# The seam between two layers: the last block's normalization moves to ScalarE, its products are shared out, and the second layer's buffers and loads are untied from the first

## The chip, the cores and the metric

The program runs on one core of a Trainium2 chip. The metric is the time of one execution in microseconds of the device. Three runs of the kernel before took 5094.03, 5087.31 and 5103.36 us; the median is 5094.03 us. Besides, one execution was recorded by the hardware profiler. Times with two decimals in the text are us from the start of its span.

In the profile PE is TensorE, DVE is VectorE, ACT is ScalarE, POOL is GpSimd and SP is SyncE, which here only issues DMAs. All work is recorded through a helper, so nearly all instructions carry its line, L158, and are told apart by the tiles that they write and read.

## The reference

The input x is 4 images of 64 channels and 256 x 256 pixels, float32. Two layers are applied, each with a group normalization ahead of it (32 groups of two channels) and a residual around it:

```
x = x + L0(group_norm(x))
x = x + L1(group_norm(x))
```

L0 raises the channels from 64 to 384 (a 1x1 convolution), runs a 3x3 depthwise convolution, and splits the result into q, k and v of 128 channels. Patches of 8 x 8 pixels of q and k are convolved circularly, `out = irfft2(rfft2(q) * rfft2(k))`. For each pixel `out` is normalized over its 128 channels: `(out - mu) / sqrt(var + 1e-5) * ln_w + ln_b`. It is multiplied by v and brought back to 64 channels.

L1 walks over the 256 columns of the image. Column w is computed from column w - 1 by a GRU cell, whose input is the three neighbouring pixels of the column before and whose state is the own column. The columns depend on each other, one after the other. The group normalization ahead of L1 needs the mean and the variance of all of layer 0's output, so nothing of L1 can be normalized before the last pixel of layer 0 is there.

## The kernel before, in words

Layer 0 works through 32 blocks (`NBLK`), each of 32 rows of one image and 64 patches per half (`NJ`). A block takes these stages, and stages of neighbouring blocks are interleaved by hand: `gated`, `project`, `add_residual` and `leave` of block n - 1 stand among the stages of block n. The order on each engine is the program's order (class `InOrder`).

- `pointwise` and `transform`: matmuls for q and k; `products` and `inverse` give `z`, the circular convolution, 128 x 64 x 128.
- `values` (eight groups, k = 0 to 7): matmuls for v into PSUM, which `keep_values` copies into the tile `v` on ScalarE: groups 0-1, 2, 3-4, 5 and 6-7. `psum(4)` and `psum()` hand out PSUM banks in a ring of eight, `place`, so a group can start only when an earlier one's copy has emptied its banks.
- `layer_norm` is a generator; `go()` runs a step of it between other stages. It takes the statistics of z, makes `mean` and `rstd` for each pixel, then scales: for each quarter of z two passes of VectorE over 128x2048 (`scaled`: subtract the mean, multiply by rstd), eight in all, and then `turned`, four transposes of z and four of v, each 128x2048.
- `gated`: ScalarE applies ln_w and ln_b to a quarter of z, and GpSimd multiplies the quarter of v by it, 128x2048.
- `project`: 32 matmuls for half a block (u = 0 or 1), summing the four quarters in PSUM.
- `residual` loads the input into slots 6 and 2 of the tile `wk` on SP's queue; `add_residual` adds it to the projection on VectorE; `leave` takes its statistics (bn_stats) and stores it to the DRAM tensor `x1` on POOL's queue.

After the loop there is a round for the last block alone (`if last:`). There `norm` is run to its end, all four quarters are gated and multiplied, and only then come, for u = 0 and again for u = 1, load, projection, add, statistics and store.

Between the layers `norm_of_blocks` combines the 32 blocks' statistics: a small reduction, a matmul with a matrix that averages (`avg4`), small operations on VectorE, a second matmul, a square root on ScalarE, a reciprocal, and a series of copies that bring mean and rstd into the two layouts that even and odd columns use (`sc1`).

The GRU's buffers are allocated after layer 0's are given back, and take their place: `raws` (16 raw columns), `xns`, `xts`, `stcols`. Layer 0's pool `big` held h, z, v, wk and other tiles together, and a tile that takes the place of a pool waits for everything that used it. `load_column` reads x1 on SP's queue, 16 columns ahead; `normalize` scales a column on ScalarE; `column` has the matmuls and `state` the gates of a column.

Of the kernel before, what the change touches and what calls it, by code (L numbers as in the profile page):

```python
# [18 lines left out]
P = 128  # L19
# [9 lines left out]
NJ = 64  # L29
# [76 lines left out]
    yield  # L106


def norm_of_blocks(nc, tmp, pool, psum, mv, eps, avg4):


    n = NBLK // B
    mean = pool.tile([P, NPAIR], F32, tag="gn1_mean", name="gn1_mean")
    rstd = pool.tile([P, NPAIR], F32, tag="gn1_rstd", name="gn1_rstd")
    m_all = tmp.tile([P, NBLK], F32, tag="m_all", name="m_all")
    d = tmp.tile([P, NBLK], F32, tag="d_all", name="d_all")
    m4 = tmp.tile([P, B], F32, tag="m4", name="m4")
    nc.vector.tensor_copy(m_all, mv[:, :, 0])
    nc.vector.tensor_reduce(
        m4, m_all.rearrange("p (b n) -> p b n", n=n), mybir.AxisListType.X, ALU.add  # L120
    )
    pm = psum.tile([P, B], F32, tag="gn", name="gn1_pm")
    nc.tensor.matmul(pm, lhsT=avg4, rhs=m4, start=True, stop=True)
    nc.vector.tensor_copy(m4, pm)
    nc.vector.tensor_tensor(
        d.rearrange("p (b n) -> p b n", n=n),
        m_all.rearrange("p (b n) -> p b n", n=n),
        m4.rearrange("p (b x) -> p b x", x=1).to_broadcast([P, B, n]),
        ALU.subtract,
    )  # L130
    nc.vector.tensor_tensor(d, d, d, ALU.mult)
    nc.vector.tensor_tensor(d, d, mv[:, :, 1], ALU.add)
    v4 = tmp.tile([P, B], F32, tag="v4", name="v4")
    nc.vector.tensor_reduce(v4, d.rearrange("p (b n) -> p b n", n=n), mybir.AxisListType.X, ALU.add)
    pv = psum.tile([P, B], F32, tag="gn", name="gn1_pv")
    nc.tensor.matmul(pv, lhsT=avg4, rhs=v4, start=True, stop=True)
    nc.scalar.activation(v4, pv, AF.Sqrt, bias=eps, scale=1.0)
    nc.vector.reciprocal(v4, v4)
    for b in range(B):
        at = slice((b % 2) * C, (b % 2) * C + C)  # L140
        nc.vector.tensor_copy(mean[at, b // 2 : b // 2 + 1], m4[at, b : b + 1])
        nc.vector.tensor_copy(rstd[at, b // 2 : b // 2 + 1], v4[at, b : b + 1])
    return mean, rstd


class InOrder:
# [17 lines left out]
def tile_conv_then_gru(  # L164
# [17 lines left out]

    const = ctx.enter_context(tc.tile_pool(name="const", bufs=1))
    dram = ctx.enter_context(tc.tile_pool(name="dram", bufs=1, space=DRAM))
    x1 = dram.tile([B, C, W, H], F32, tag="x1", name="x1")


    t_all = dram.tile([3, ROWS, 8, 16 * NS], F32, tag="t_all", name="t_all")
# [22 lines left out]
    st1 = const.tile([P, NBLK, 2], F32, tag="st1", name="st1")  # L211
    st1 = const.tile([P, NBLK, 2], F32, tag="st1", name="st1")
    with layer0 as s:
        big = s.enter_context(tc.tile_pool(name="big", bufs=1))
        tp = s.enter_context(tc.tile_pool(name="tp", bufs=4))
        ps2 = s.enter_context(tc.tile_pool(name="ps2", bufs=1, space=PSUM))
# [6 lines left out]
            place[0] = (at + banks) % 8  # L223
            return ring[:, at % 8 : at % 8 + banks]

        hx = big.tile([P, P * NP], F32, tag="h", name="h")
        h = hx[0:HALO].rearrange("p (c n) -> p c n", n=NP)
        z = big.tile([P, NJ, E], F32, tag="z", name="z")
        v = big.tile([P, NJ, E], F32, tag="v", name="v")
# [237 lines left out]
        def keep_values(k, count, pv):  # L467
            nc.scalar.copy(
                v[:, :, 16 * k : 16 * (k + count)], pv.rearrange("p x (f n) -> p n (x f)", n=NJ)
            )  # L470

        def layer_norm(n):

            st = lnst[:, 0:384].rearrange("p (a i k) -> p a i k", a=2, k=6)
# [37 lines left out]
                    )  # L512
                    yield

            def turned(of, i):
                chunk = of[:, :, 32 * i : 32 * i + 32]
                nc.vector.transpose(chunk, chunk)

            for i in range(4):
                yield from scaled(i)  # L520
            for i in range(4):
                turned(z, i)
                yield
                turned(v, i)
                yield

        def gated(n, i):
            f = slice(32 * i, 32 * i + 32)
            nc.scalar.activation(
                z[:, :, f],  # L530
                z[:, :, f],
                AF.Identity,
                bias=ln_sb[:, 1, i : i + 1],
                scale=ln_sb[:, 0, i : i + 1],
            )
            nc.gpsimd.tensor_tensor(v[:, :, f], v[:, :, f], z[:, :, f], ALU.mult)

        bn = {}

        def residual(n, u):  # L540
            b, r0 = n // 8, (n % 8) * 32 + u * 8
            xr = [wk[:, i].rearrange("p (r c) -> p r c", c=P) for i in (6, 2)]
            for g in range(2):
                for s in range(2):
                    nc.sync.dma_start(
                        xr[g][s * C : (s + 1) * C],
                        x[b, :, r0 + 16 * g : r0 + 16 * g + 8, s * P : s * P + P],
                    )
            return xr
# [26 lines left out]
                        ALU.add,  # L576
                    )

        def leave(n, u, xr):

            b, r0 = n // 8, (n % 8) * 32 + u * 8
            if u == 0:
                bn[n] = big.tile([P, 8, 6], F32, tag="bn", name=f"bn_{n}")
            for g in range(2):
                flat = xr[g].rearrange("p r c -> p (r c)")
                for p in range(2):
                    nc.vector.bn_stats(bn[n][:, 4 * u + 2 * g + p, :], flat[:, p * 512 : (p + 1) * 512])
                for s in range(2):
                    nc.gpsimd.dma_start(
                        x1[b, :, r0 + 16 * g : r0 + 16 * g + 8, s * P : s * P + P],  # L590
                        xr[g][s * C : (s + 1) * C],
                    )
            if u == 1:
                nc.vector.bn_aggr(st1[:, n, :], bn.pop(n))
# [22 lines left out]
        for n in range(NBLK + 1):  # L617
            last = n == NBLK
            more = not last and n // 8 + 1 < B
            if last:  # L620
                for _ in norm:
                    pass
                for i in range(4):
                    gated(n - 1, i)
                for u in range(2):
                    xr = residual(n - 1, u)
                    add_residual(u, project(n - 1, u), xr)
                    leave(n - 1, u, xr)
                break
            if more:  # L630
                look(n, 0)
# [51 lines left out]
            for unit in range(16):  # L683
                pointwise(n, 2, unit, unit in (4, 6, 15))
                if more and unit == 2:
                    count(n, 12)
                    if n % 8 == 7:
                        t = wk[:, 3]
                        nc.gpsimd.dma_start(t[:, 0 : 2 * P].rearrange("p (a q) -> p a q", a=2), sums)
                        image = norm_of_pieces(nc, st0, t, lambda: psum()[:, :, 0], eps, sc0[:, n // 8 + 1])  # L690
                if image and unit in (4, 8, 12):
                    next(image)
                if unit == 3:
                    flush()
                if unit in (6, 7):
                    go()
                if unit % 4 == 3 and n + 1 < NBLK:
                    load(n + 1, unit // 4)
            po = project(n - 1, 1) if n else None
            go(1)  # L700
            if n:
                add_residual(1, po, xr[1])
            go(3)
            for k in range(8):
                if k in (0, 3, 6):
                    pv = psum(4)
# [8 lines left out]
                if k in (1, 2, 4) and n + 1 < NBLK:  # L715
                    normalize(n + 1, k // 2)
                if k == 5 and n:
                    leave(n - 1, 1, xr[1])
                if k == 5 and n + 1 < NBLK:
                    normalize(n + 1, 3)  # L720
                if k in (6, 7):
                    go()
            fetch(n * 24 + 28)


# [11 lines left out]
    b_rz = l1c.tile([P, 2], F32, tag="b_rz", name="b_rz")  # L737
    nc.vector.tensor_tensor(b_rz, bias_sb[:, 0:2], bias_sb[:, 3:5], ALU.add)
    nc.vector.tensor_scalar(b_rz[:, 1:2], b_rz[:, 1:2], -1.0, None, ALU.mult)
    with tc.tile_pool(name="stb", bufs=1) as stb, tc.tile_pool(name="gnps1", bufs=1, space=PSUM) as gnps:  # L740
        avg4 = stb.tile([P, P], F32, tag="avg4", name="avg4")
        nc.scalar.dma_start(avg4, avg2)
        mean1, rstd1 = norm_of_blocks(nc, stb, l1c, gnps, st1, eps, avg4)

        sc1 = l1c.tile([P, 2, NPAIR, 2], F32, tag="sc1", name="sc1")
        nc.vector.scalar_tensor_tensor(sc1[:, 0, :, 0], mean1, -1.0, rstd1, ALU.mult, ALU.mult)
        nc.vector.tensor_copy(sc1[:, 0, :, 1], rstd1)
        for slot in range(2):
            for half in range(2):
                b = SLOTS[1][slot][half]  # L750
                nc.vector.tensor_copy(
                    sc1[half * C : (half + 1) * C, 1, slot], sc1[(b % 2) * C : (b % 2) * C + C, 0, b // 2]
                )

    WB = 8
    with ExitStack() as s:
# [5 lines left out]

        def column_parts(m, w):

            raw = raws[w]
            if w % 2 == 0:
                yield m[:, :, w, :].rearrange("(k a) c h -> (a c) k h", k=NPAIR), raw
            else:
                for half in range(2):
                    b0 = SLOTS[1][0][half]  # L770
                    yield m[b0 : b0 + 2, :, w, :].rearrange("b c h -> c b h"), raw[half * C : half * C + C]

        def load_column(w):
            raws[w] = rawp.tile([P, 2, H], F32, tag="raw", name=f"raw_{w}")
            for of, to in column_parts(x1, w):
                nc.sync.dma_start(to, of)

        def new_columns(n):
# [196 lines left out]
```

## Time and profile before

| | |
|---|---|
| median of three runs | 5094.03 us |
| the profiled execution's own time | 5097.92 us |
| its span, first to last instruction | 5096.1 us |
| mean granted TensorE clock | 0.993 |
| busy: PE, DVE, ACT, POOL | 95%, 79%, 65%, 34% |
| last matmul of layer 0's values | ends at 3676.2 |
| first matmul of the GRU's columns | starts at 3732.01 |
| last gated product on GpSimd | ends at 3702.36 |
| raw<-x, the first column load | lands at 3730.1 |

How to read it: the span is cut into 40 slices of 127 us in the page; a digit is the share of a slice in tenths, 9 is 90% or more. In a timeline or a chain a line begins with its start and its length in us. "xN" is the number of instructions that a line merges. In brackets stands the idle time of the engine before it and what ended it. A group's row ends with busy us, the mean ns of one instruction, and the idle time ahead of them.

### The profile page before, as it was taken

How to read it: one execution, taken by the hardware profiler on the slowest of the kernel's cores; microseconds unless marked ns; L12 is line 12 of the kernel's file. 1: busy time of each engine (PE TensorE's matmuls, PEld its weight loads, DVE VectorE, ACT ScalarE, POOL GpSimd, SP SyncE). 2: the span in 40 equal slices, each digit the busy share in tenths (PEclk: the TensorE clock that was granted, in tenths of full speed). 3: DMA queues.
4: the chain of work that ended last, by engine and by line, in shares of the span. 5: the costliest groups of instructions: out<-in, count | busy, mean ns of one | idle time of the engine just before them, and what ended most of it. 6: DMA issues, size and time to landing. Idle time of an engine off the chain costs nothing.

```text
span 5096.1 us, 276113 instructions
## 1 busy us (share of the span) xinstructions
PE 4858.1 (95%) x127092; PEld 4237.7 (83%) x127092; DVE 4035.9 (79%) x7001; ACT 3317.3 (65%) x4269; POOL 1727.2 (34%) x1717
## 2 busy tenths in 40 slices
PE   6999999999999999999999999999879999999999
PEld 4888888888888888888888888888669999999998
DVE  5788888877888888788888877778867777777777
ACT  4666666666666666666666666666556666666665
POOL 0233333333333334333333333323343333333333
PEclk9999999999999999999999999999989999999999
DMA  8577676676777667677676666666443333333332
GB/s 306 162 189 191 186 191 182 180 183 187 187 195 196 170 184 187 179 190 191 186 195 168 173 161 174 173 171 180 121 125 103 104 103 103 102 104 103 103 103 73
DMA packets 435056, 823.57 MB, mean 162 GB/s; under 512 B 37156, under 2 KB 300068, under 8 KB 431364
## 3 DMA queue, kind: packets, MB, share of 16 engines
q1 hardware_dynamic: 380600, 582.13, 43.3%
q0 software_dynamic: 52432, 223.12, 14.7%
q8 instruction: 997, 16.33, 1.4%
q14 instruction: 163, 1.34, 0.1%
q10 hardware_dynamic: 864, 0.66, 0.0%
HBM read 660.53 MB, written 145.23 MB: 158 GB/s over the span
## 4 chain that ended last, share of the span: by engine, by line
PE 87%; ACT 4%; issue 4%; DVE 3%; DMA 2%; POOL 1%; SPq 0%; POOLq 0%; ACTq 0%; DVEq 0%
PE psring L158 62%; PE pshr L158 9%; PE pshz L158 8%; PE psni L158 6%; PE pshn L158 2%; ACT v L158 1%; ACT z L158 1%; DVE wk L158 1%; ACT xq L158 1%; DMA t<-t_all 1%; DVE z L158 1%; DMA t_all<-wk 0%; DVE lnst L158 0%; ACT h L158 0%; POOL v L158 0%
## 5 line engine op out<-in xcount | busy, mean ns | idle before, releaser
L158 PEld LDWEIGHTS psring<-h,t 100*32 100x32 f32 x49152 | 1385.9, 119 | 251.6 <-issue 214.5
L158 PE MATMUL psring<-h,t 100*32 100x128 f32 x49152 | 1463.5, 257 | 104.2 <-issue 69.4
L158 PEld LDWEIGHTS psring<-w_sb,xq 64*100 64x100 f32 x24576 | 1358.6, 163 | 107.9 <-issue 76.5
L158 PE MATMUL psring<-w_sb,xq 64*100 64x128 f32 x24576 | 1412.4, 271 | 23.0 <-issue 8.7
L158 ACT COPY h<-psring 100x1024 f32<-100x1024 f32 (+2 forms) x1371 | 1231.5, 990 | 308.0 <-PE psring L158 307.4
L158 DVE TENSOR_TENSOR wk<-psring,wk 128x1024 f32<-128x1024 f32 (+1 forms) x768 | 759.5, 1037 | 480.1 <-PE psring L158 346.4
L158 POOL TENSOR_TENSOR v<-v,z 128x2048 f32<-128x2048 f32 x128 | 582.9, 4558 | 664.5 <-DVE wk L158 603.5
L158 DVE TENSOR_TENSOR z<-z,moments 128x2048 f32<-128x2048 f32 x256 | 578.0, 2278 | 2.3
L158 POOL TENSOR_TENSOR wk<-wk 128x1024 f32<-128x1024 f32 x128 | 303.5, 2371 | 622.3 <-DVE wk L158 607.9
L158 POOL TENSOR_TENSOR raw<-raw,st 128x512 f32<-128x512 f32 x256 | 303.2, 1184 | 540.1 <-DVE st L158 424.6
L158 ACT COPY z<-psring 128x2048 f32<-128x2048 f32 (+1 forms) x144 | 248.4, 1725 | 343.9 <-PE psring L158 262.6
L158 ACT ACTIVATE z<-pshz,b_rz 128x288 f32<-128x288 f32 (+7 forms) x510 | 242.1, 475 | 339.2 <-PE pshz L158 334.1
L158 ACT COPY wk<-psring 128x1024 f32<-128x1024 f32 (+1 forms) x272 | 268.9, 988 | 288.5 <-PE psring L158 237.1
L158 PE MATMUL pshr<-st,wi 64*64 64x144 f32 (+7 forms) x12240 | 448.8, 270 | 6.9 <-DVE st L158 6.5
L158 PE MATMUL pshz<-st,wi 64*64 64x144 f32 (+7 forms) x12240 | 444.2, 269 | 0.9 <-issue 0.9
L158 PE MATMUL psni<-st,wi 64*64 64x144 f32 (+7 forms) x12240 | 444.0, 269 | 0.1
L158 DVE COPY h<-psring 100x1024 f32<-100x1024 f32 (+1 forms) x230 | 278.1, 1210 | 191.9 <-PE psring L158 188.1
L158 PEld LDWEIGHTS pshr<-st,wi 64*64 64x64 f32 x12240 | 378.0, 133 | 49.7 <-DVE st L158 36.9
L158 ACT COPY v<-psring 128x2048 f32<-128x2048 f32 (+2 forms) x176 | 251.9, 1436 | 254.3 <-PE psring L158 254.3
L158 DVE BATCH_NORM_STATS2 lnst<-z 128x6 f32<-128x128 f32 x2048 | 416.8, 281 | 0.0
L158 PEld LDWEIGHTS psni<-st,wi 64*64 64x64 f32 x12240 | 389.4, 133 | 21.9 <-issue 0.2
L158 PE MATMUL psring<-wk,g_sb 32*64 32x512 f32 x6144 | 386.7, 599 | 15.1 <-issue 12.1
(91 smaller groups left out, 6258.4 us busy)
## 6 DMA issues: line engine op xcount, KB each, us to landing
t<-t_all SPq DMA_DIRECT2D x768, 448.0 KB, 4.6
xq<-in_xh POOLq DMA_DIRECT2D x124, 800.0 KB, 5.2
wk<-in_x SPq DMA_DIRECT2D x256, 256.0 KB, 8.1
x<-wk POOLq DMA_DIRECT2D x256, 256.0 KB, 5.0
wk<-in_x POOLq DMA_DIRECT2D x96, 512.0 KB, 6.9
raw<-x SPq DMA_DIRECT2D x128, 256.0 KB, 3.0
raw<-x SPq DMA_DIRECT2D x256, 128.0 KB, 3.1
out<-raw SPq DMA_DIRECT2D x128, 256.0 KB, 2.7
```

What stands on the lines that cost most here:

```text
L158: return self.tc.keep_in_program_order(got(*args, **kwargs))
```

## The change

It has five parts, of which four touch only the last block and the seam.

1. `hx`, the tile h, gets a pool of its own (`hp`), ahead of `big`.
2. x1 is eight DRAM tensors of 32 columns each instead of one, so that a column load depends on the stores of its own eighth.
3. For the last block `layer_norm` makes `total = -mean * rstd` and scales z on ScalarE, one patch index k at a time: 64 activations of 128x128 with bias and scale by address, in eight steps of eight, which `go()` spreads over the groups of values. The transposes of v are put between the groups; those of z are made in halves (patches 0 to 31 and 32 to 63).
4. In the last round gates and products are made in halves: three products of the first half on GpSimd, the fourth and all four of the second half on VectorE. Each half is projected as soon as its products are there. The residual's loads of the last block are issued earlier, into slots 1 and 5 and into 6 and 2, and block 30's second store goes to SP's queue. Both adds come ahead of both sets of statistics.
5. `norm_of_blocks` reads the means in place, writes its results straight into one tile for four images (`sc4`), which four copies bring into `sc1`, and has a one-element Sigmoid activation after the square root, so that the table of functions for the GRU is loaded there.

```diff
-def norm_of_blocks(nc, tmp, pool, psum, mv, eps, avg4):
+def norm_of_blocks(nc, tmp, psum, mv, eps, avg4, sc):
...
-    nc.vector.tensor_copy(m_all, mv[:, :, 0])
...
     nc.scalar.activation(v4, pv, AF.Sqrt, bias=eps, scale=1.0)
-    nc.vector.reciprocal(v4, v4)
-    for b in range(B):
-        at = slice((b % 2) * C, (b % 2) * C + C)
-        nc.vector.tensor_copy(mean[at, b // 2 : b // 2 + 1], m4[at, b : b + 1])
-        nc.vector.tensor_copy(rstd[at, b // 2 : b // 2 + 1], v4[at, b : b + 1])
-    return mean, rstd
+    nc.scalar.activation(d[:, 0:1], eps, AF.Sigmoid, bias=eps, scale=1.0)
+    nc.vector.reciprocal(sc[:, :, 1], v4)
+    nc.vector.scalar_tensor_tensor(sc[:, :, 0], m4, -1.0, sc[:, :, 1], ALU.mult, ALU.mult)
...
-    x1 = dram.tile([B, C, W, H], F32, tag="x1", name="x1")
+    x1 = [dram.tile([B, C, 32, H], F32, tag=f"x1_{i}", name=f"x1_{i}") for i in range(W // 32)]
...
+        hp = s.enter_context(tc.tile_pool(name="hp", bufs=1))
...
-        hx = big.tile([P, P * NP], F32, tag="h", name="h")
+        hx = hp.tile([P, P * NP], F32, tag="h", name="h")
...
+        def turned(of, i, n0=0, n1=NJ):
+            chunk = of[:, n0:n1, 32 * i : 32 * i + 32]
+            nc.vector.transpose(chunk, chunk)
...
+            if n < NBLK - 1:
...
+                return
+            nc.vector.scalar_tensor_tensor(total, mean, -1.0, rstd, ALU.mult, ALU.mult)
+            for k in range(NJ):
+                nc.scalar.activation(
+                    z[:, k, :], z[:, k, :], AF.Identity, bias=total[:, k : k + 1], scale=rstd[:, k : k + 1]
+                )
+                if k % 8 == 7:
+                    yield
...
-        def leave(n, u, xr):
+        def leave(n, u, xr, queue=nc.gpsimd):
...
-                for i in range(4):
-                    gated(n - 1, i)
-                for u in range(2):
-                    xr = residual(n - 1, u)
-                    add_residual(u, project(n - 1, u), xr)
-                    leave(n - 1, u, xr)
+                m, po = n - 1, []
+                for i in range(4):
+                    turned(z, i, 0, 32)
+                    if i < 3:
+                        gated(m, i, 0, 32)
+                turned(v, 3)
+                for i in range(4):
+                    turned(z, i, 32, 64)
+                gated(m, 3, 0, 32, nc.vector)
+                po.append(project(m, 0))
+                for i in range(4):
+                    gated(m, i, 32, 64, nc.vector)
+                po.append(project(m, 1))
+                for u in range(2):
+                    add_residual(u, po[u], xrs[u])
+                for u in range(2):
+                    leave(n - 1, u, xrs[u])
                 break
...
+            if n == NBLK - 1:
+                xrs = [residual(n, 0, (1, 5))]
             po = project(n - 1, 1) if n else None
...
                 if k == 5 and n:
-                    leave(n - 1, 1, xr[1])
+                    if n < NBLK - 1:
+                        leave(n - 1, 1, xr[1])
+                    else:
+                        leave(n - 1, 1, xr[1], nc.sync)
+                        xrs.append(residual(n, 1))
...
+                if n == NBLK - 1 and k < 5:
+                    go()
+                if n == NBLK - 1 and k in (3, 6, 7):
+                    turned(v, (3, 6, 7).index(k))
...
-            for of, to in column_parts(x1, w):
+            for of, to in column_parts(x1[w // 32], w):
```

## The prediction

> **What bounds the kernel now.** I read the page's slices first, then the chain of waits over the seam between the two layers, then the rows of each engine there, and SP's own waits.
>
> ```profile
> PE   6999999999999999999999999999879999999999
> ...
> PEclk9999999999999999999999999999989999999999
> ```
>
> ```profile
> SPq L158 <- DMA x<-wk: 50.0, 4, 37.5
> ```
>
> TensorE is busy in every slice but the first and the pair where layer 0 gives way to the GRU; layer 0 and the GRU columns are TensorE's and the diff leaves them alone. All of it happens in that dip, so the price is that of one seam. The other line is from SP's own waits: there its queue stands for 37.5 us behind one store of x1. The chain of waits over the seam (start us, us, what) shows what sets its length:
>
> ```profile
> 3675.28 2.21 DVE z L158
> ...
> 3681.96 2.28 DVE v L158
> ...
> 3684.40 4.29 POOL v L158
> ...
> 3702.41 6.12 PE psring L158 x80
> 3708.52 14.49 issue
> ...
> 3727.32 2.80 DMA raw<-x
> ...
> 3730.38 0.68 ACT xn L158 x2
> ...
> 3732.01 1.11 PE pshr L158 x2
> ```
>
> VectorE scales z until 3679.8 and begins to transpose, GpSimd then makes four products in a row (4.45 each, until 3702.36), TensorE projects until 3708.3. The 14.49 us of "issue" are the second residual load, its adds and statistics: TensorE waits for the normalization, which comes at 3723. Last come the column loads, which could not start before everything of the last block had left. The last matmul of the convolution ended at 3676.2, the GRU's first starts at 3732.0: 55.8 us.
>
> Three rows of ScalarE's timeline (start, us), GpSimd's group of 128x1024 products (busy, mean ns), and two stretches (us, then PE, PEld, DVE, ACT, POOL busy, clock, DMA share):
>
> ```profile
> 3730.38 4.25 ACT L158 ACTIVATE xn<-raw,sc 128x256 f32<-128x256 f32 x8 [4.70 <-DMA raw<-x]
> 3734.64 1.28 ACT L158 ACT_TABLE_LOAD   x1
> 3736.74 0.50 ACT L158 ACTIVATE g<-pshr,b_rz 128x288 f32<-128x288 f32 x1 [0.81 <-PE pshr L158]
> ```
>
> ```profile
> L158 POOL TENSOR_TENSOR wk<-wk 128x1024 f32<-128x1024 f32 x128 | 303.5, 2371 | 622.3 <-DVE wk L158 607.9 <-PE psring L158 14.5
> ```
>
> ```profile
> 3678.00:3709.00 31.00, 11.98 (x128) 2.94 (x128) 23.96 (x17) 8.50 (x5) 20.55 (x8) 0.56 0.06 12
> 3709.00:3732.00 23.00, 1.15 (x4) 1.00 (x4) 9.32 (x35) 1.89 (x5) 3.56 (x6) 0.57 0.68 168
> ```
>
> The reader is to see that ScalarE has room (8.50 of 31 us), that DMA is nearly idle (0.06) while the products are made, and that TensorE's clock is halved once it idles.
>
> **The change part by part.** All times are on the trace's clock.
>
> *Scaling on ScalarE.* Eight passes of VectorE (18.0 us in this stretch) go; one bias instruction (0.23) and 64 activations of 128x128 come. No row has that form. From below: an activation of 128x64 with one operand by address took 347 ns, less an overlap of 0.1 with the next. From above: xn, 128x256, two operands by address, 591 ns. The x2 rows of xn take 1.08, so one starts 0.495 after the other; xq (1600 elements, 1725 ns) and z (2048, 2096) give 0.83 ns an element; 128 fewer leave 0.389 us. I take that, as it is xn's form: 64 x 0.389 = 24.9 us. Ends: 0.25 and 0.59.
>
> These stand in ScalarE's queue between the copies that empty PSUM for the last eight groups of values, so each copy is late, and TensorE with it. The ring gives groups 0-1 banks 0-3, group 2 banks 4-5, groups 3-4 banks 0-3, 5 banks 4-5, 6-7 banks 0-3. The bias is ready at 3657.0. Sixteen patches end at 3663.3, the copy (1.87) at 3665.1, eight patches 3668.2, copy (1.01) 3669.3, sixteen 3675.5, copy 3677.3, eight 3680.5, copy 3681.5. Groups 6 and 7 may start at 3677.3 only. At the 2.0 us a group that TensorE needs (325 of 512 records in 10.04 us) they end at 3681.3; TensorE had then stood idle 6 us, and the clock was halved 2 us after the values ended, so I take 3683. Copy to 3685.0, last sixteen patches to 3691.2. VectorE was through at 3679.8: this part alone is 11.4 us late. (At 0.25 a patch no group of values is held up, ScalarE ends at 3682.4, and all that follows GpSimd's first product comes 8.8 earlier.)
>
> The Trainium skill ("ScalarE: Activation LUTs", section "Rules for kernel authors") says to do additions and multiplications on VectorE, not ScalarE. The rows agree as to engine time (24.9 against 18.0), and by that rule alone the edit loses 6.9 us; what it leaves out is that VectorE also has the transposes.
>
> *What VectorE does meanwhile.* Three of four transposes of v are over by 3683.7 (v 2 waits for the copy at 3681.5, 2.27 us each), four half transposes of z (2.27 / 2 = 1.1 each) by 3688.2, v 3 by 3690.4, the other halves, waiting for the last patches, from 3691.2 to 3695.7. So 18.2 us of transposes, on the path before, hide behind the patches.
>
> *Gates and products.* Gates are now eight halves: 2.09 less 1024 elements at 0.83 ns is 1.24, so the first ends at 3692.4, and with xn's overlap of 0.1 one more each 1.14 us. GpSimd takes three halves. Row: 2.37 us for a product of 128x1024; half of 4.45 would be 2.23; I take the row: 3692.5 to 3699.6, instead of 17.95 us for four whole ones. VectorE's five, at half of a 2.28 pass each, are bound by the gates: fourth of the first half at 3697, last of the second at 3701.6. They are beside GpSimd's and before TensorE needs them.
>
> *Projection.* Of both halves a quarter takes 2.02 us at the cold clock, 0.92 warm (3.69 for four). After 3699.6 two quarters of the first half and four of the second are left: the trace's last five quarters took 5.93, cold at first, so six take 5.5 to 6.8. Here TensorE rests only 0.35 us between quarters, not 2.4; I take 6.1: end 3705.7 (before: 3708.3).
>
> *Residual.* Its eight loads move: four ahead of a matrix load at 3638.8 on SP (they wait for the inverse's matmuls, 3642.6, then 3.8 us; that matrix is used at 3665, covered), four behind the store of the block before, which moves from POOL's queue to SP's. SP thus passes its 37.5 us wait; loads land by about 3681 and are used after 3701. The adds of the second half start 0.4 before the projection's end, 4 x 0.6, then eight statistics 8 x 0.6 in a row: aggregation starts at 3712.6. Before: 3722.0. **Gain 9.4.** The last stores (0.7 us each on POOL, 4.2 to landing) end near 3713, before their readers at 3717.
>
> *Normalization.* From the aggregation's start to the end of the square root 3.64 us before; the copy of the means goes (0.2). Fifteen small VectorE operations after the root (2.1 us) give way to six (the same rows: about 1.1), and beside them stands the table load with a one-element Sigmoid, pulled ahead: 1.28 + 0.3. It thus costs 0.5 here and returns nothing where it was, for g waited for TensorE there (0.81). First xn at 3712.6 + 3.64 - 0.2 + 1.58 = 3717.6; before it was 8.35 after the aggregation. **Gain 3.3**, and it exists only since x1 in eight tiles and h in its own pool let the 24 column DMAs be issued from 3683 on, once h is read (15 us on SP, long landed). The Trainium skill ("ScalarE: Activation LUTs", section "What ACT_TABLE_LOAD costs") adds a drain of 1.38 us to a load of 1.28; the trace shows the load and at most 0.81 after it. By the page the sum would be 1.4 us smaller.
>
> *First columns.* One TensorE stall of 0.93 us ("issue", at 3745) came while column loads kept the DMA engines full; with the loads done it may go. Bounds 0 to 0.9; I take 0.8. The GRU's order is otherwise unchanged.
>
> **Sum:** 9.4 + 3.3 + 0.8 = 13.5 us, 0.27%. The profiled execution took 5097.9 (span 5096.1), 3.9 above the median of the three runs; 5084.4 by it, 5080.5 by the median.
>
> **The rivals.**
> - *TensorE stays warm.* If groups 6-7 restart at full clock (-2), the projection goes warm at once (-0.6), products take 2.23 (-0.4), and VectorE's queue allows (-0.5): gain 17, 5077. For: the gaps shrink. Against: the window of 31 us has clock 0.56.
> - *Dear patches.* At 0.591 each, no overlap: 64 x 0.2 = 12.9 more, gain 0.6: 5093. Against: the x2 rows overlap.
> - *Slower.* The same place: ScalarE's queue makes copies and TensorE wait for patches. From 0.60 a patch it eats the whole gain, from 0.84 the kernel is over 0.3% slower (5109). For: 64 instructions each with its own bias and scale; against: twice as long as xn's row is needed.
> - *Columns are not early.* If the first column still waits for the stores, the 3.3 go: 5084.
>
> **How the numbers follow.** A measurement of this kernel can tell about 0.3%, 15.3 us, from no change; the three runs lie 16 us apart. Forecast 0.50 (its own range 5076 to 5085, scatter of the runs puts 0.22 beyond 0.3%), warm 0.30 (beyond), dear patches 0.08 and late columns 0.05 (within), slower 0.07. Faster 0.52, same 0.41, slower 0.07. The range goes from a gain of 23 (patches at the low end, 13.5 + 8.8, or warm with the scatter) to one of 5 (half of what the dear patches cost, with the page's drain).
>
> **What would show it.** Right: 64 z activations about 0.39 apart between 3657 and 3691; values ending near 3683, not 3676; three GpSimd products of about 2.3 us; no SP wait on x<-wk of tens of us; first GRU matmul near 3719 (shift 13). Wrong: a patch over 0.45, a GpSimd product over 2.6 beside VectorE's, a gap between the table load and xn, or column loads issued after 3710.

## The result, and the profile after

Twenty runs of the changed kernel have a median of 5085.85 us, twenty of the kernel before 5094.49 us. The medians lie 8.6 us apart. The ratio of the runs, which is not that of the two medians, is 0.9979, with a 95% interval of 0.997 to 0.9989: a gain of 5.6 to 15.3 us, 10.7 in the middle. The forecast was 5080.5 us, a gain of 13.5, inside a range of 5071 to 5089. The profiled execution took 5082.58 us, its span is 5080.8.

One execution differs from the next by more than the edit is worth, and most of that arises before the seam: in the recorded traces below, the last block's statistics are ready anywhere between 3644.7 and 3667.6 us, and the GRU takes 1361.5 to 1369.1. So everything below is counted from one event that each trace has: the start of VectorE's reciprocal in the last block's `layer_norm` (3656.21 in the trace of before, 3653.68 in that of after). From there to the first GRU matmul is "the seam". It took 75.80 us before and takes 64.82 now: 10.98 less. The first eight columns, counted from there to the first matmul of the ninth, take 45.28 us instead of 46.44.

| us after the reciprocal | before | predicted | after |
|---|---|---|---|
| last patch scaled | 23.6 (VectorE) | 35.0 | 34.91 |
| last matmul of the values | 20.02 | 26.8 | 26.82 |
| GpSimd's last product | 46.14 | 43.4 | 44.07 |
| VectorE's last product | none | 45.4 | 48.56 |
| projection ends | 52.13 | 49.5 | 49.73 |
| aggregation starts | 65.82 | 56.4 | 58.13 |
| last store of x1 lands | 68.5 | 56.8 | 62.73 |
| first xn | 74.17 | 61.4 | 63.18 |
| first GRU matmul | 75.80 | 63.1 | 64.82 |

The predicted column is the prediction's own times, less 3656.21; its total gain of 13.5 is 12.7 here and 0.8 in the columns.

The page's slices of the changed kernel, the same two rows as before:

```profile
PE   6999999999999999999999999999889999999999
...
PEclk9999999999999999999999999999989999999999
```

The dip at the seam is still there. SP's own waits in the changed kernel (what it waited for: us in total, times, longest):

```profile
SPq L151 <- DMA avg<-in_avg: 10.5, 1, 10.5
...
SPq L151 <- DMA x<-wk: 1.2, 2, 0.7
```

The 37.5 us behind one store are gone, as forecast. A wait that nobody forecast stands in their place, 10.5 us behind a load that is ScalarE's.

The chain of waits over the seam (start us, us, what):

```profile
3660.86 1.75 ACT v L151
...
3666.60 6.17 ACT z L151 x16
...
3678.54 2.31 DVE v L151
3680.85 3.39 DVE z L151 x3
3684.25 9.05 ACT z L151 x16
3693.42 1.87 DMA avg<-in_avg
...
3699.13 4.78 DMA raw<-x
3703.97 0.68 DVE wk L151
...
3708.70 7.71 DMA x<-wk
3717.37 1.08 ACT xn L151 x2
3718.50 1.61 PE pshr L151 x4
```

In place of VectorE's passes, GpSimd's four products and 14.49 us of "issue" stand ScalarE's patches (z) and copies (v), then loads, adds and the last store of x1: xn starts 0.45 us after that store has landed (3708.70 + 7.71), at 3716.86. The chain's way over the averaging matrix and the column loads is no bound: by the timeline below, VectorE's adds start right behind its products.

The timeline of the changed kernel, single rows of ScalarE, TensorE, VectorE and GpSimd (start, us, engine, operation; in brackets the idle time ahead):

```profile
3654.59 6.27 ACT L151 ACTIVATE z<-z,lnst,moments 128x128 f32<-128x128 f32 x16 [0.94 <-DVE lnst L151]
...
3715.21 1.28 ACT L151 ACT_TABLE_LOAD   x1
3716.51 0.29 ACT L151 ACTIVATE d_all<-eps 128x1 f32<-128x1 f32 x1
...
3723.72 0.50 ACT L151 ACTIVATE g<-pshr,b_rz 128x288 f32<-128x288 f32 x1 [2.81 <-PE pshr L151]
...
3674.57 5.94 PE L151 MATMUL psring<-h,t 100*64 100x64 f32 x128 [5.83 <-ACT v L151]
...
3697.81 5.61 PE L151 MATMUL psring<-v,wo_sb 32*64 32x512 f32 x96 [1.45 <-POOL v L151]
...
3693.18 9.07 DVE L151 TENSOR_TENSOR v<-v,z 128x1024 f32<-128x1024 f32 x5
3702.17 4.86 DVE L151 TENSOR_TENSOR wk<-psring,wk 128x512 f32<-128x512 f32 x8
3706.96 4.83 DVE L151 BATCH_NORM_STATS2 bn<-wk 128x6 f32<-128x512 f32 x8
...
3689.80 7.95 POOL L151 TENSOR_TENSOR v<-v,z 128x1024 f32<-128x1024 f32 x3 [51.09 <-ACT z L151]
```

Sixteen patches take 6.27 us and one alone 0.48, so they follow each other at (6.27 - 0.48) / 15 = 0.386. TensorE waits 5.83 us for the copy of v before the last two groups of values. VectorE's five products take 9.07 us; its eight adds, the eight statistics and the aggregation follow without a pause. The two products' own rows (min/median/max in ns) show how:

```profile
L151 DVE TENSOR_TENSOR v<-v,z x5: 1210/1212/3364, 3693.2 to 3701.0; 128x1024 f32<-128x1024 f32 x5
...
L151 POOL TENSOR_TENSOR v<-v,z x3: 2355/2357/3336, 3689.8 to 3694.4; 128x1024 f32<-128x1024 f32 x3
```

Alone, a product takes VectorE 1.21 us and GpSimd 2.36. Where they meet, two of VectorE's take 2.38 and 3.36, one of GpSimd's 3.34.

### The profile page after: what moved, and what is told of

It is laid out like the page before. It is cut to its first block, busy times and chain, and to the rows that moved or that the text cites. A ratio compares the mean times of both kernels' runs of the same rounds, so it can differ in the third digit from the quotient of the medians.

```text
span 5080.8 us, 276166 instructions
## 1 busy us (share of the span) xinstructions
PE 4859.1 (96%) x127092; PEld 4231.3 (83%) x127092; DVE 4024.5 (79%) x6993; ACT 3344.8 (66%) x4338; POOL 1717.6 (34%) x1712
## 3 DMA queue, kind: packets, MB, share of 16 engines
q14 instruction: 164, 1.34, 0.1%
## 4 chain that ended last, share of the span: by engine, by line
PE 87%; ACT 5%; issue 4%; DMA 2%; DVE 2%; POOL 0%; SPq 0%; POOLq 0%; ACTq 0%; DVEq 0%
PE psring L151 62%; PE pshr L151 9%; PE pshz L151 8%; PE psni L151 6%; PE pshn L151 2%; ACT z L151 2%; ACT v L151 2%; ACT xq L151 1%; DMA t_all<-z 1%; DMA t<-t_all 0%; DVE wk L151 0%; DVE lnst L151 0%; ACT h L151 0%; POOL wk L151 0%; DVE n L151 0%
## 5 line engine op out<-in xcount | busy, mean ns | idle before, releaser
L151 POOL TENSOR_TENSOR v<-v,z 128x2048 f32<-128x2048 f32 (+1 forms) x127 | 573.3, 4518 | 686.2 <-DVE wk L151 596.8
L151 DVE TENSOR_TENSOR z<-z,moments 128x2048 f32<-128x2048 f32 x248 | 559.8, 2277 | 2.2
L151 PE MATMUL psni<-st,wi 64*64 64x144 f32 (+7 forms) x12240 | 433.6, 269 | 0.0
L151 PE MATMUL pshz<-st,wi 64*64 64x144 f32 (+7 forms) x12240 | 433.5, 269 | 0.0
L151 PEld LDWEIGHTS pshr<-st,wi 64*64 64x64 f32 x12240 | 367.5, 133 | 54.6 <-DVE st L151 38.7
L151 PEld LDWEIGHTS psni<-st,wi 64*64 64x64 f32 x12240 | 376.9, 133 | 26.7
```

The costliest lines, as they stand in the source:

```text
L151: return self.tc.keep_in_program_order(got(*args, **kwargs))
```

## The experiments

Two theories stood against each other. The prediction's: ScalarE takes the scaling off VectorE, whose transposes thereby hide behind the patches, and that with the earlier residual makes the seam shorter. The rival, formed on the trace of after: the patches hold TensorE and the copies up for as long as they relieve VectorE, so moving the scaling is worth nothing, and the gain is that of the other parts. Single total times of one kernel lie up to 25 us off its median, so of the kernels that ran only once the seam alone is read.

### Scaling back on VectorE

```diff
-            nc.vector.scalar_tensor_tensor(total, mean, -1.0, rstd, ALU.mult, ALU.mult)
-            for k in range(NJ):
-                nc.scalar.activation(
-                    z[:, k, :], z[:, k, :], AF.Identity, bias=total[:, k : k + 1], scale=rstd[:, k : k + 1]
-                )
-                if k % 8 == 7:
-                    yield
+            for i in range(4):
+                yield from scaled(i)
```

> Changed kernel with the last block's z scaled by VectorE again (eight passes, one per step), all else kept. Seam = from the start of the last block's reciprocal on VectorE to the first GRU matmul: 75.8 us before, 64.8 in the changed kernel. Theory A (the patches on ScalarE hold up the values and end the scaling 11 us later, and what they gain is only that VectorE's transposes run beside them): values end about 20 after the reciprocal instead of 26.8, GpSimd's first product starts near 32 instead of 36.1, VectorE's products end near 47 instead of 48.6, seam about 63.4. Theory B (moving the scaling off VectorE is where the gain comes from): 18 us of VectorE return to the path, seam 74 or more.

Measured: seam 63.84, 0.98 shorter than in the changed kernel. The values end at 18.21, the transposes at 41.29 instead of 39.57, but the products at 46.93 instead of 48.56. The timeline of this run, GpSimd's and VectorE's products:

```profile
3698.07 6.98 POOL L151 TENSOR_TENSOR v<-v,z 128x1024 f32<-128x1024 f32 x3 [47.54 <-ACT z L151]
...
3706.71 5.72 DVE L151 TENSOR_TENSOR v<-v,z 128x1024 f32<-128x1024 f32 x5
```

GpSimd is through at 3705.05, 1.66 us before VectorE starts, and the same five products take 5.72 us instead of 9.07. They are over 1.63 us earlier, of which 0.65 is lost again between the aggregation and xn (5.70 us instead of 5.05). The theory that the move to ScalarE pays falls: with all else kept, the seam is no longer without it.

### All products on GpSimd, all products on VectorE

In the first run every `gated` of the last round goes to GpSimd:

```diff
-                gated(m, 3, 0, 32, nc.vector)
+                gated(m, 3, 0, 32)
...
-                    gated(m, i, 32, 64, nc.vector)
+                    gated(m, i, 32, 64)
```

> Changed kernel with all eight half products on GpSimd. Theory A: eight at 2.35 in a row from 36.1 after the reciprocal end at 55, against 48.6; the adds of the second half start near 57, seam about 70.5. Theory B (VectorE's products at 1.8 us are no gain over GpSimd, since they slow GpSimd as much): seam within 1 us of 64.8.

Measured: the eight products end at 54.66, the seam is 70.51, both as the first theory has them. In its timeline GpSimd's products stand in one unbroken row:

```profile
3698.98 18.41 POOL L151 TENSOR_TENSOR v<-v,z 128x1024 f32<-128x1024 f32 x8 [51.23 <-ACT z L151]
```

Giving work to VectorE is thus worth 5.7 us of the seam. In the second run VectorE takes all eight and GpSimd none. With `None`, `gated` makes the activation alone; `multiplied` is its product, put into a function of its own:

```diff
...
                 for i in range(4):
                     turned(z, i, 0, 32)
-                    if i < 3:
-                        gated(m, i, 0, 32)
+                    gated(m, i, 0, 32, None)
                 turned(v, 3)
                 for i in range(4):
                     turned(z, i, 32, 64)
-                gated(m, 3, 0, 32, nc.vector)
+                for i in range(4):
+                    multiplied(i, 0, 32, nc.vector)
                 po.append(project(m, 0))
```

> Changed kernel with all eight half products on VectorE and none on GpSimd. Theory A (a product on VectorE and one on GpSimd at the same time hold each other up): each takes 1.2 us, all eight end near 48.7 after the reciprocal, as five did beside GpSimd's three, and the seam stays within 1 us of 64.8. Theory B (such a product takes VectorE 1.8 us in itself): they end near 54 and the seam is about 70.

Measured: seam 64.98, 0.16 from the changed kernel's. The row of its products:

```profile
L151 DVE TENSOR_TENSOR v<-v,z x8: 1182/1218/1220, 3688.5 to 3696.4; 128x1024 f32<-128x1024 f32 x8
```

Eight products alone take VectorE 9.13 us; five beside GpSimd's three took 9.07. GpSimd's three products bring nothing where the change puts them: what they take off VectorE, VectorE loses beside them.

### The residual loaded late

Both halves of the last block's residual use the same slots again, each loaded, added, measured and stored before the next:

```diff
-            if n == NBLK - 1:
-                xrs = [residual(n, 0, (1, 5))]
...
-                        xrs.append(residual(n, 1))
...
                 for u in range(2):
-                    add_residual(u, po[u], xrs[u])
-                for u in range(2):
-                    leave(n - 1, u, xrs[u])
+                    xr = residual(m, u)
+                    add_residual(u, po[u], xr)
+                    leave(m, u, xr)
```

> As the changed kernel, but the last block's residual is loaded as before: both halves into the same slots, the second after the first half's sum has left, and each half is added, measured and stored before the next. Theory A (the prediction's, that this load was the 14.49 us of the old chain): first half's statistics until 53.3, its stores land at about 57, second loads land at about 62, adds and statistics until 66.5, xn 71.6, seam 73: 8 to 9 us more than 64.8. Theory B (the chain would be bound by VectorE's products anyway): seam at most 67.

Measured: seam 73.91. VectorE's timeline:

```profile
3697.09 2.46 DVE L151 BATCH_NORM_STATS2 bn<-wk 128x6 f32<-128x512 f32 x4
3706.13 1.29 DVE L151 TENSOR_TENSOR wk<-psring,wk 128x512 f32<-128x512 f32 x2 [6.59 <-DMA wk<-in_x]
3708.76 1.29 DVE L151 TENSOR_TENSOR wk<-psring,wk 128x512 f32<-128x512 f32 x2 [1.34 <-DMA wk<-in_x]
3709.96 2.46 DVE L151 BATCH_NORM_STATS2 bn<-wk 128x6 f32<-128x512 f32 x4
```

VectorE waits 6.59 and 1.34 us for the second load, and the seam is 9.1 us longer, 8.57 of it before the aggregation. (The column loads come late in this run too, behind that load on SP's queue: the first at 58.6.) The 14.49 us of "issue" in the old chain were indeed the wait for this load, with its adds and statistics: most of the gain of 10.98 hangs on it. (The amounts of the runs do not add up to the gain, for the parts cover each other.)

### One tensor x1, h back in the large pool

```diff
-    x1 = [dram.tile([B, C, 32, H], F32, tag=f"x1_{i}", name=f"x1_{i}") for i in range(W // 32)]
+    x1 = dram.tile([B, C, W, H], F32, tag="x1", name="x1")
...
-        hx = hp.tile([P, P * NP], F32, tag="h", name="h")
+        hx = big.tile([P, P * NP], F32, tag="h", name="h")
```

> Changed kernel with x1 as one tensor and h in the pool with z, v and wk, so that no column load is issued before the last stores have landed. Theory A (the stores land late in the changed kernel because the column loads run beside them, and the table load stands on the path anyway, so early columns buy little): stores land about 3 us earlier, loads are issued near 60 after the reciprocal, first xn near 63.8, seam about 65.4, and the first eight columns take about 1 us longer. Theory B (the prediction's: early columns are worth 3.3 us): seam about 68.

Measured: the column loads start at 61.3 instead of 26.9, the last store lands at 60.9 instead of 62.7. From the aggregation to xn it is 5.83 us instead of 5.05, the first eight columns take 46.59 instead of 45.28. The seam is 66.76, but 1.15 of its 1.94 us more were lost before the aggregation, to a projection at half the clock (below). Rows of its timeline, SP and ScalarE:

```profile
3721.13 14.36 SPq L151 DMA_DIRECT2D raw<-x  x21
...
3724.95 4.17 ACT L151 ACTIVATE xn<-raw,sc 128x256 f32<-128x256 f32 x8 [0.85 <-DMA raw<-x]
```

Early columns are worth 0.8 us at the seam and 1.3 in the first columns, 2.1 us in all. The first column by itself follows the clock (below); columns 2 to 8 take 39.28 us here and 37.19 in the changed kernel.

So only 0.8 of the 3.3 us from the aggregation to xn hang on these two parts. SP's waits in the trace of before show another piece:

```profile
SPq L158 <- DVE gn_rstd L158: 1.8, 1, 1.8
```

There the column loads started at 3726.87, after the normalization's last copies and 2.1 us after the last store had landed. The normalization's temporaries stood in a pool of their own (`stb`), given back just before the raw columns were allocated; the change moves them into `l1c`, which stays, though the list of its parts does not say so. In this run that move is kept, and the loads start 0.4 us after the last store. The move was not undone alone.

### SP's new wait, and the early table load

In the trace of after, SP issues seven column loads from 26.9 on and then stands until 41.6, when the averaging matrix, loaded on ScalarE's queue, has landed. SP does not use that matrix. Two runs bear on it and on the Sigmoid; the first has one line changed, the second leaves the Sigmoid out too:

```diff
-        nc.scalar.dma_start(avg4, avg2)
+        nc.sync.dma_start(avg4, avg2)
```

> As the changed kernel, but the matrix for the layer's averages is loaded on SyncE's queue, ahead of the raw columns, and no longer on ScalarE's. In the changed kernel eight raw loads go out at 26.9, and then SP stands until 41.6 and the rest land beside the stores of x1, whose last takes 7.7 us. Theory A (the column loads, late by that stall, slow the stores, and xn waits for the stores): SP issues all 24 raw loads without a stall of 10 us, they land before 50, the last store takes 4 to 5 us instead of 7.7, xn starts right after the table load (62.8) and the seam is 64.4 instead of 64.8. Theory B (the stores are slow by themselves): they still take 7 to 8 us, xn and seam within 0.2 of 63.2 and 64.8.

Measured: all 24 loads go out without the stall. SP's timeline in the changed kernel:

```profile
3680.60 28.96 SPq L151 DMA_DIRECT2D raw<-x  x24
```

and in this run:

```profile
3695.04 15.26 SPq L151 DMA_DIRECT2D raw<-x  x24
```

The last store takes 6.3 us instead of 7.7, less of a gain than the 4 to 5 expected. From the aggregation to xn it is 4.89 us instead of 5.05. The seam is 65.13: the 0.16 is gained, but the values ended 0.5 later in this run. Neither theory is hit squarely; the stall is worth about 0.2 us.

```diff
-    nc.scalar.activation(d[:, 0:1], eps, AF.Sigmoid, bias=eps, scale=1.0)
```

> As the run before, and without the one-element Sigmoid, so that the table load stands before the first g of the GRU again. Theory A (the early table load is on the path, and where it was it was hidden by TensorE): xn starts at the later of the scales (62.2) and the last store's landing, the seam is 0.5 to 1 us shorter than with it, and the first column is no longer than 8.1 us: in the changed kernel g waited 2.8 us for TensorE after xn. Theory B (the load costs the same wherever it stands): the seam 1.3 shorter, the first column 1.3 longer.

Measured: from the aggregation to xn 4.32 us instead of 4.89, the first eight columns 46.43 instead of 45.65. So the early load costs 0.57 and returns 0.78, or more: the first column takes 9.30 us here, and 8.03 and 8.09 in the split kernel below and the changed one, where the clock came back as long after the first matmul (4.7 to 4.9 us). ScalarE's rows in this run:

```profile
3735.69 1.28 ACT L150 ACT_TABLE_LOAD   x1 [2.74 <-PE pshr L150]
3736.99 0.50 ACT L150 ACTIVATE g<-pshr,b_rz 128x288 f32<-128x288 f32 x1
```

The load stands behind the wait for TensorE, not ahead of it as in the trace of before, so it is not hidden. Why it stands there is not shown. The first theory's earlier xn came true; its unchanged first column (8.1) did not: it took 9.30, about the 1.3 more of the second theory. The seam of this run, 66.14, is longer, for the projection ended at 52.88 at half the clock.

### The scaling split

With the scaling worth nothing on ScalarE alone and GpSimd worth nothing beside VectorE, a kernel follows: VectorE scales patches 0 to 31 in two passes, ScalarE 32 to 63; GpSimd takes the four products of the first half while VectorE still transposes, VectorE those of the second. The transposes of z's first half and of v now stand between the groups of values and right behind them (in hunks not printed), and the averaging matrix is loaded on SP's queue.

```diff
...
+            if n == NBLK - 1:
+                for part, what in ((0, ALU.subtract), (1, ALU.mult)):
+                    nc.vector.tensor_tensor(
+                        z[:, 0:32],
+                        z[:, 0:32],
+                        moments[:, part, 0:32].rearrange("p (n x) -> p n x", x=1).to_broadcast([P, 32, E]),
+                        what,
+                    )
...
-            for k in range(NJ):
+            for k in range(NJ // 2, NJ):
...
                 for i in range(4):
                     turned(z, i, 32, 64)
-                gated(m, 3, 0, 32, nc.vector)
+                for i in range(4):
+                    gated(m, i, 0, 32)
                 po.append(project(m, 0))
                 for i in range(4):
                     gated(m, i, 32, 64, nc.vector)
```

> VectorE scales the patches 0 to 31 in two passes, ScalarE only the patches 32 to 63, one at a time, between its copies; GpSimd takes the four products of the first half, VectorE those of the second; the averaging matrix on SyncE's queue. Theory A (the 64 patches on ScalarE hold TensorE up as long as they relieve VectorE, and what counts is the sum on VectorE): values end at about 20 instead of 26.8, VectorE's products end at 37 to 38, aggregation starts at about 47.5, seam 54, some 10 us shorter than 64.8. Theory B (the gates on ScalarE or GpSimd's four products become the bound): products end at 43 or later, seam 60 or more.

Measured: seam 53.63, values end at 17.39, products at 37.49. The timeline, VectorE and GpSimd:

```profile
3656.22 8.87 DVE L151 TENSOR_TENSOR z<-z,moments 128x4096 f32<-128x4096 f32 x2
...
3681.06 4.58 DVE L151 STREAM_TRANSPOSE z<-z 128x1024 f32<-128x1024 f32 x4
3685.56 4.59 DVE L151 TENSOR_TENSOR v<-v,z 128x1024 f32<-128x1024 f32 x4
...
3675.57 9.26 POOL L151 TENSOR_TENSOR v<-v,z 128x1024 f32<-128x1024 f32 x4 [37.88 <-ACT z L151]
```

GpSimd's products (2.32 to 2.36 each) lie beside transposes, which are no slower for it (4.58 for four), and VectorE's come after them at 1.15 each. Both kernels were then timed on one chip:

> The split kernel again, timed. Its seam was 53.6 us against 75.8 before and 64.8 in the changed kernel, and the first columns are 1.7 shorter than before. Theory A (the seam's length is all that differs, the rest is scatter): 23.9 us less than before, 0.47%: ratio 0.9953, 5070.6 us. Theory B (what the seam gains is lost again in the GRU): ratio 0.998 or more.

> The changed kernel again, timed beside the split one on the same chip. Theory A: by its seam (64.8 against 75.8) and 1.7 in the first columns, 12.7 us less than before, 0.25%: ratio 0.9975, 5081.8 us; 11.2 us more than the split kernel. Theory B (the gain comes from the chip or the rounds): ratio 0.999 or more.

| | median us | ratio to before | interval | seam |
|---|---|---|---|---|
| before | 5095.48 | | | 75.80 |
| changed, again | 5083.23 | 0.9978 | 0.9964 to 0.9991 | 65.88 |
| split | 5062.69 | 0.9947 | 0.993 to 0.9964 | 53.62 |

The seam of before is that of the first trace. The changed kernel's gain came again. The split one gains 27 us by its ratio (18 to 36); the medians lie 32.8 apart. The 23.9 expected lie inside, though they count 1.7 us in the first columns, where the traces show 1.2. Between the two the medians differ by 20.5 us; the seams account for 12.3. Of the profiled executions, the split one had also reached its reciprocal 5.5 us earlier (3644.72 against 3650.20); whether the edit has a part in that is not settled.

### The clock at the projection

The changed kernel's second trace has a longer seam (65.88) with the same products (to 48.13). TensorE's rows there, the projections of the first half's first two quarters and of the six that are left:

```profile
3688.30 2.01 PE L151 MATMUL psring<-v,wo_sb 32*64 32x512 f32 x16 [11.71 <-POOL v L151]
3690.61 2.02 PE L151 MATMUL psring<-v,wo_sb 32*64 32x512 f32 x16 [0.30 <-POOL v L151]
3693.89 8.37 PE L151 MATMUL psring<-v,wo_sb 32*64 32x512 f32 x96 [1.27 <-POOL v L151]
```

The same 96 matmuls took 5.61 in the first trace. Stretches of both, first of the changed kernel's first trace, then of its second (us, then PE, PEld, DVE, ACT, POOL busy, clock, DMA share, GB/s):

```profile
3692.20:3696.10 3.90, 3.59 (x32) 0.66 (x32) 3.90 (x3) 3.90 (x4) 3.90 (x2) 0.51 0.06 17
3696.10:3699.80 3.70, 2.25 (x48) 0.97 (x48) 3.70 (x2) 1.55 (x2) 1.65 (x1) 1.00 0.66 195
```

```profile
3688.30:3694.60 6.30, 4.73 (x40) 1.00 (x48) 6.30 (x3) 5.43 (x5) 5.54 (x2) 0.50 0.26 75
3694.60:3699.90 5.30, 5.30 (x56) 1.67 (x48) 5.30 (x7) 0.00 (x0) 0.08 (x1) 0.50 0.69 205
```

In the first the clock is full from 3696.1, 3.9 us after the projection began; in the second only from 3699.9, 11.6 us after. Of the seven traces that scale all patches on ScalarE and have VectorE through with its products at 48.1 to 49.1, the projection ended between 49.5 and 50.2 in four (the first trace, all on VectorE, matrix on SP, late residual) and between 52.0 and 52.9 in three (second trace, one x1, late table).

The GRU's first column shows the clock too. With its loads early and the table loaded early it takes, for instance, 7.57, 7.83, 8.09, 8.32 and 8.66 us where the full clock came 3.62, 4.33, 4.86, 5.65 and 6.32 us after its first matmul (all on VectorE, second trace, first trace, matrix on SP, all on GpSimd).

## Why the prediction was right, and where not

The total and its sign were right, and most of the steps: the sum of 12.7 us at the seam came out as 10.98 in one trace and 9.9 in another. It had put 0.52 on a gain that can be told from no change, which it set at 0.3%, and 0.41 on a smaller one; the 0.21% measured is the smaller one. What it missed by is mainly one term, VectorE's products.

- **Patches.** 0.389 us each was taken from xn's overlapped rows; a row of sixteen gives 0.386. The end, 35.0, was 34.91. The stall that they bring to TensorE, "idle 6 us" before the last groups, was 5.83. Rival "dear patches" and the slower one die here.
- **What the scaling is worth.** The numbers of that step held, its sense did not. The prediction said that the Trainium skill's rule to keep multiplications and additions on VectorE ("ScalarE: Activation LUTs", section "Rules for kernel authors") leaves out the transposes. With the scaling back on VectorE the seam was 0.98 us shorter: the rule held for this kernel, and what is shown to pay in the package are VectorE's products (5.7) and the residual (9.1); the halves were not run alone. In the split kernel, where each engine scales half, the seam is 10 to 11 us shorter than in either; but GpSimd's share and the transposes lie elsewhere there too, and how much is due to which was not separated.
- **VectorE's products: the mis-sized term.** "VectorE's five, at half of a 2.28 pass each", through at 45.4, was taken from rows in which GpSimd stood still. They were through at 48.56. Nor were they "bound by the gates", which were over at 43.97. The prediction looked for the damage at GpSimd ("over 2.6 beside VectorE's"), and one of its three did take 3.34; but two of VectorE's lost 1.17 and 2.15 us. The consequence is the 1.7 us by which the aggregation came late: the prediction had the first half's four adds over before the projection's end and only four left (4 x 0.6); with VectorE busy until 48.56, all eight followed in a row (4.86 us). Five runs bear this out: here, with the scaling or all products on VectorE, with the matrix on SP and in the split kernel the aggregation starts 9.57 us after VectorE's last product, wherever that lies between 37.49 and 49.04.
- **Projection.** The 6.1 us came out as 5.61 in the first trace, begun 0.7 later than predicted; that its end fits (49.73 for 49.5) is luck, for it is a matter of the clock: 8.37 for the same matmuls in the second. The prediction's upper end, 6.8, was too low. The rival "TensorE stays warm" did not come: the clock was halved from 18.5 on, while the last values were still to come.
- **Residual.** The largest term, 9.4 to the aggregation, was 7.69; its cause is shown by the late residual (8.57 longer up to there). The 1.7 us that are missing are those of VectorE's products.
- **Normalization.** 3.3 was predicted from the aggregation to xn, and 8.35 - 5.05 = 3.30 measured. The reason given for it was wrong: it "exists only since x1 in eight tiles and h in its own pool" let the loads go early, but with both put back 2.5 of the 3.3 stay (5.83). The prediction had read the old column loads as waiting for the last block to leave; they waited for the normalization's last copies too (1.8 us). That those copies are no longer waited for is part of the rest; how the 2.5 are made up was not separated. The cover was thinner than thought: the last store took 7.7 us to land, not 4.2, beside the column loads, and held xn up by about 0.15 (5.05 here, 4.89 where it did not). In the run with all products on VectorE it cost 0.76 (5.65). "Returns nothing" was wrong for the table load: it returns 0.78 or more in the first column. A drain of 1.38 us, which the Trainium skill adds to a table load ("ScalarE: Activation LUTs", section "What ACT_TABLE_LOAD costs") is not seen: the next activation starts at 3716.51, 0.02 after the load's end.
- **SP.** The old wait went, a new one came (10.5 us), which the prediction didn't list among the queues. It was nearly covered (0.2).
- **First columns.** 0.8 predicted, 1.16 measured, but of two parts. The first column takes 8.09 us instead of 7.61, with the clock back 4.9 us after its first matmul instead of 4.0; columns 2 to 8 take 37.19 instead of 38.82, and 37.1 to 37.3 in every run whose loads are early. The stall of 0.93 us is gone, as forecast; the other 0.7 us was not foreseen.

## What to carry to other kernels

A price for one engine from a row in which its neighbour idles does not hold once both work: when products of two operands in SBUF are shared out between VectorE and GpSimd, put GpSimd's beside work of VectorE that doesn't collide (here the transposes), or give them all to VectorE. Moving work to an idle engine bought nothing here, where that engine's queue also feeds another (the copies that empty PSUM); half of it, laid between those copies, with GpSimd's share moved beside the transposes, shortened the seam by 11 us. For an edit worth 0.2% whose runs lie 0.5 to 0.8% apart, measure the stretch between two events of the same trace, and the total only with many runs.

## What the runs showed of the hardware

- **Products of VectorE and GpSimd take turns.** In the trace of after, GpSimd's second product ends at 3694.47 and VectorE's first, begun at 3693.18, at 3695.55, 1.08 later; GpSimd's third, begun at 3694.42, ends at 3697.75, 2.20 after that; VectorE's second at 3698.84, 1.09 after that. Each ends about one product's own length after the other's end. The Trainium skill ("SBUF — State Buffer", section "Who interferes with whom") has this rule: the port pair that the two engines share is an exclusive lock, and a VectorE instruction with two inputs in SBUF contends with a GpSimd instruction that reads SBUF. The numbers here agree with it; the prediction's 45.4 let the products of both engines run side by side. Transposes (one input) of 1.14 us beside GpSimd's products were not slowed.
- **A queue can wait for another queue's load that it doesn't use.** SP's eighth column load stood 10.5 us for a DMA of ScalarE's queue; with that DMA on SP's own queue the stall was gone. The trace shows why: the load on ScalarE's queue and SP's eighth column load tell of their landing by the same semaphore (110), and SP waits for it before it issues; the column loads use eight semaphores in turn.
- **TensorE's clock comes back in steps.** In both traces of the changed kernel the clock changes at intervals that are multiples of 3.41 us. In the first it is halved at 18.48 us after the reciprocal, full at 25.31, halved at 28.72, full at 42.37 and halved at 52.61: 6.83, 3.41, 13.65 and 10.24 us apart, so 2, 1, 4 and 3 times 3.41. In the second it is halved at 22.42, full at 25.84, halved at 29.25, full at 49.73 and halved at 56.56: 1, 1, 6 and 2 times. The projection began at half the clock in both, and got the full clock 3.9 us later in one and 11.6 in the other, with the first two quarters fed at the same pace (0.30 us between them). Why it came so much later in the second is not shown.
